# Paged attention with conditioned input: the second tile's mix and key projection moved ahead of the third query projection, its spreads and the output weights put in other slots

## The chip, the cores and the metric

The kernel runs on one core of one Trainium2 chip. A core has a matrix engine (TensorE, PE in the profile, with its weight loads as PEld), a vector engine (DVE), a scalar engine (ACT), GpSimd (POOL) and a sync engine (SP) that here only issues transfers. Each has its own instruction queue, and semaphores tie them together. The metric is the device time of one execution in microseconds; less is better.

## The reference

The input x has 64 sequences of 32 tokens with 512 features. The reference adds two residual branches. In the first, each sequence picks one of 16 matrices of 32 x 32 by its condition, and its 32 tokens are mixed with it:

```python
W = weights[condition]
x = x + einsum('bct,bcd->bdt', x, W)
```

The second is attention with a paged cache, 32 query heads and 8 key/value heads of 128 elements, 512 cached positions per sequence:

```python
q, k, v = x @ Wq.T, x @ Wk.T, x @ Wv.T         # 32, 8 and 8 heads
q, k = rope(rmsnorm(q, q_norm_w), pos), rope(rmsnorm(k, k_norm_w), pos)
k_all = concat(k_cache[block_table], k)         # 512 cached + 32 new keys
v_all = concat(v_cache[block_table], v)
o = softmax(mask(q @ k_all.T / sqrt(128))) @ v_all
x = x + o @ Wo.T
```

All is in float32.

## The kernel before, in words

The 2048 tokens are cut into 16 tiles of 128 tokens, which are four sequences ("batches" in the code) each. The heads are cut into two halves of 4 key heads and 16 query heads. So there are 32 steps, `steps[0]` to `steps[31]`: tiles 0 to 15 for the first half, then the same tiles for the second half (steps 16 to 31; the texts call them tiles 16 to 31). In the first half a step mixes its tile (`x1_c`, a matmul with the block-diagonal `bd`, and an add into `acc`), transposes it (`x1_b`) and stores the transposed tile `x1t` in DRAM; in the second half it is loaded again (`x1_t`).

From `x1t` come five kinds of projection, each of eight matmul instructions of 512 columns (`project`, line 401): one for the keys (`k_a`), one for the values (`v_a`) and four for the queries (`q_a`, one for each key head of the half). `norm_rope` then normalizes and rotates on ACT (square), DVE (six operations) and POOL (a power), with tables made by `rot_tables` from `cos` and `sin`. `angles` makes the latter for two tiles at a time, on DVE and ACT; its sine takes another function table on ACT than the exponential. The result goes into `rows`. For the first tile PE transposes `rows` into `q_cols` and `q_last` (`q_b`, `k_b`), and ACT copies; for all others DVE turns the rows (line 451) and SP spreads them by transfers within the chip's buffer (`spread`, line 465, four transfers per batch). `q_cols` holds batches 0 to 2 of a tile and `q_last`, of which there are two, batch 3.

For each batch, SP loads 16 key pages (`load_k`, line 291, two buffers), POOL gathers the values (line 315), DVE or ACT copies the keys of one head together (`head_keys`, `kh`), PE computes scores (line 570), ACT the exponential `pr`, and PE the values' sum (line 628). The 32 new keys of each sequence are done for a whole tile: `new_scores` (line 588, `psn`), their exponential `pn` on ACT, and `new_values` (line 612, `pnv`), which ACT copies into `nv`. `turn` (line 659) turns the finished batch into `ot`, and `out_proj` (line 516) multiplies it with the output weights `wo`, in slots 8 and 9 of the next tile.

A tile has 16 slots, four batches times four heads. A slot takes PE about 1.8 us with scores and values alone, and about 5.2 us with a projection. In each slot the loop of lines 901 to 976 also does a piece of the next tile, by the table of `pieces`, and loads weights part by part. The order of instructions of SP and PE is the order of the program throughout (line 88). In the opening, up to line 859, that holds for all engines; behind it a scheduler orders DVE, ACT and POOL. The opening computes the first tile's projections, the first batch and the start of the second, and puts the second tile's first pieces between them.

Buffers that matter here: the projections' PSUM pool `ps_p` has four buffers, used in turn by all that is named "pp" (mix, transposes, projections, new scores, new values, output projection). Every wait of a transfer issued by SP or ACT includes one for the transfer eight places earlier, since eight semaphores are used in turn.

Of the kernel before, what the change touches and what calls it, by code (L numbers as in the profile page):

```python
# [19 lines left out]
P = 128  # L20
# [7 lines left out]
BT = P // S  # L28
# [27 lines left out]
def cond_resid_paged_attention_kernel(  # L56
# [130 lines left out]
    def steps_of(exact, pools):  # L187
# [148 lines left out]
        class Step:  # L336
            def __init__(self, n):
                self.n, self.hh, self.t = n, n // NT, n % NT
                self.name = f"{n}_{uid}"

        def x1_a(st):

            st.acc = work.tile([P, HID], F32, tag="acc", name=f"acc_{st.name}", bufs=3)
            src = acc_d[st.t] if st.hh else x[st.t * P : (st.t + 1) * P, :]
            nc.sync.dma_start(st.acc, src)
# [14 lines left out]
        def x1_b(st):  # L360
            if st.hh:
                return
            pm = ps_p.tile([P, KC, P], F32, tag="pp", name=f"px1t_{st.name}")
            for c in range(KC):
                nc.tensor.transpose(pm[:, c, :], st.acc[:, c * P : (c + 1) * P], ident)
            st.x1t = work.tile([P, KC, P], F32, tag="x1t", name=f"x1t_{st.name}", bufs=1)
            nc.scalar.copy(st.x1t, pm)
            nc.scalar.dma_start(x1t_d[st.t], st.x1t.rearrange("p c q -> p (c q)"))

        def rot_tables(st):  # L370

            st.rot = {}
            c, s = cos[:, st.t, :], sin[:, st.t, :]
            for name, w in norm_w.items():
                cw = work.tile(
                    [P, 2, HD],
                    F32,
                    tag=f"cw_{name}",
                    name=f"cw_{name}_{st.name}",
                    bufs=1,  # L380
                )
                sw = work.tile(
                    [P, 2, HD],
                    F32,
                    tag=f"sw_{name}",
                    name=f"sw_{name}_{st.name}",
                    bufs=1,
                )
                w1, w2 = w[:, 0:HD], w[:, HD:D]
                nc.gpsimd.tensor_tensor(cw[:, 0, :], w1, c, ALU.mult)  # L390
                nc.gpsimd.tensor_tensor(cw[:, 1, :], w2, c, ALU.mult)
                nc.vector.scalar_tensor_tensor(
                    sw[:, 0, :], w2, -1.0, s, ALU.mult, ALU.mult
                )
                nc.gpsimd.tensor_tensor(sw[:, 1, :], w1, s, ALU.mult)
                st.rot[name] = cw, sw
# [379 lines left out]
        load_w("q", 0, 1, eng=nc.gpsimd)  # L776
        batch = Batch(first, 0)
        load_w("q", 0, 2)
        load_w("v", 0)
        x1_a(second)  # L780
# [28 lines left out]
        trig = work.tile([P, 3, TRIG * HD], F32, tag="w1", name="trig1", bufs=1)  # L809
        angles(TRIG, trig)  # L810
# [5 lines left out]
        q_a(first, 1)  # L816
        q_b(first, 0)
        head_keys(batch, 0, nc.scalar)
        head_keys(batch, 1, nc.scalar)
# [5 lines left out]
        k_b(first)  # L825
        for c in (0, 1):
            batch.fill(c)
            fetch(1, c)
        v_a(first)
        q_b(first, 1)  # L830
        x1_c(second)
# [7 lines left out]
        x1_b(second)  # L839
# [3 lines left out]
        rot_tables(second)  # L843
        k_a(second)
        q_b(first, 3)
        v_a(second)
# [4 lines left out]
        values(batch, 1)  # L851
        new_values(first, 2)
# [8 lines left out]
        def pieces(st):  # L861
            do = {
# [10 lines left out]
            if st is second:  # L873
                do[2] = do[3] = do[13] = ()
            return do
# [10 lines left out]
        new_ot(first)  # L886
# [13 lines left out]
        load_cond_weights(2)  # L900
        for st in steps:
# [3 lines left out]
            for bt in range(0 if st.n else 1, BT):  # L905
# [5 lines left out]
                for g in range(GH):  # L911
# [16 lines left out]
                    if slot == 9:  # L928
                        if st.n:
                            new_ot(st)  # L930
# [24 lines left out]
                    if st.t < 2:  # L955
                        load_parts([("o", i) for i in range(GH)], st.hh, slot - 10 + st.t * BT * GH)
# [95 lines left out]
```

## Time and profile before

| what | value |
|---|---|
| median of three runs | 2204.2 us (2204.06 to 2207.32) |
| the profiled execution's own time | 2204.06 us |
| its span from first to last instruction | 2202.3 us |
| PE busy | 2156.6 us (98%) |
| DVE, ACT, POOL busy | 1198.1, 867.5, 806.1 us |
| mean granted clock of PE | 0.991 of full speed |
| key loads `k_t` | 2048 of 64 KB |
| output weight loads `wo` | 32 of 256 KB |
| moved by all transfers | 358.77 MB, 163 GB/s over the span |

In a line of waits, the columns are the engine and what it wanted to run, what released it, and then the total in us, the number of waits and the longest. In a timeline line, the columns are the start in us, the duration (or how long a group of equal instructions lasted), the engine, the line of the code, the operation, its output and inputs, and how many; square brackets hold the idle time just before and what ended it. SPq is the queue of SP, which issues transfers. Names end in x where the program numbers them.

### The profile page before, as it was taken

The page shows a single profiled execution, that of the slowest core. Times are in us where ns is not written, and L with a number is a line of the kernel's source. Part 1 is how long each engine was busy: PE and PEld are TensorE (multiplying, and loading weights), DVE is VectorE, ACT ScalarE, POOL GpSimd, SP SyncE. Part 2 cuts the span into 40 slices and gives each one's busy share as a digit, 9 for nine tenths or more (in the row PEclk, how much of TensorE's full clock was granted, in tenths as well). Part 3 has the DMA queues.
Part 4 walks back from the last instruction along what each step waited for, and adds up shares of the span by engine and source line. Part 5 has one row for each costly group of instructions (what it writes and reads, how often), then busy time and mean ns, then how long its engine had stood idle before and what let it go on. Part 6 is the DMA issues. An engine that isn't in the chain of part 4 may idle for free.

```text
span 2202.3 us, 41557 instructions
## 1 busy us (share of the span) xinstructions
PE 2156.6 (98%) x12970; PEld 1502.4 (68%) x12970; DVE 1198.1 (54%) x2881; ACT 867.5 (39%) x1574; POOL 806.1 (37%) x1008
## 2 busy tenths in 40 slices
PE   8889999999999999999999999999999999999998
PEld 5657766677766777666776567776667776667775
DVE  5545466655555654565554555445656445656442
ACT  3424444444333444333433244333334433334441
POOL 4423243333333433333333343334333334334330
PEclk9989999999999999999999999999999999999999
DMA  7575554555555555556766655655555655555551
GB/s 226 160 177 168 159 155 143 165 157 171 155 151 151 158 168 162 154 147 197 238 176 174 165 167 162 176 158 154 148 163 163 174 159 158 149 162 158 174 158 55
DMA packets 387863, 358.77 MB, mean 163 GB/s; under 512 B 54737, under 2 KB 316897, under 8 KB 387633
## 3 DMA queue, kind: packets, MB, share of 16 engines
q1 hardware_dynamic: 342912, 215.10, 34.9%
q0 software_dynamic: 41712, 136.66, 20.9%
q10 hardware_dynamic: 3008, 4.25, 0.5%
q8 instruction: 106, 1.74, 0.3%
q14 instruction: 125, 1.02, 0.2%
HBM read 302.59 MB, written 12.58 MB: 143 GB/s over the span
## 4 chain that ended last, share of the span: by engine, by line
PE 93%; DMA 3%; SPq 2%; issue 1%; ACT 1%; DVE 0%; POOL 0%; DVEq 0%; ACTq 0%; POOLq 0%
PE po_x L628 20%; PE pout_x L516 20%; PE ps_x L570 20%; PE pp_q_x L401 19%; PE pp_k_x L401 5%; PE pp_v_x L401 5%; PE pnv_x L612 2%; PE psn_x L588 1%; SPq L291 1%; DMA k_t_x<-in_kt_dram 1%; PE pmix_x L357 1%; DMA raw_x<-in_vc_dram,v_row 0%; DMA x1t_d<-x1t_x 0%; DMA x1t_x<-x1t_d 0%; DMA wq_x<-in_wq_dram 0%
## 5 line engine op out<-in xcount | busy, mean ns | idle before, releaser
L315 POOL DMA_INDIRECT raw_x<-in_vc_dram,v_row x512 | 538.8, 1052 | 837.9 <-ACT v_x L328 769.3
L578 ACT ACTIVATE pr_x<-ps_x 128x512 f32<-128x512 f32 x512 | 305.8, 597 | 837.4 <-PE ps_x L570 774.4
L628 PEld LDWEIGHTS po_x<-v_x,pr_x 128*128 128x128 f32 x4096 | 516.5, 192 | 125.5 <-issue 114.8
L628 PE MATMUL po_x<-v_x,pr_x 128*128 128x129 f32 x4096 | 551.8, 278 | 0.9 <-ACT v_x L328 0.6
L401 PE MATMUL pp_q_x<-wq_x,x1t_x 128*128 128x512 f32 x1024 | 465.0, 597 | 2.8 <-DMA wq_x<-in_wq_dram 2.8
L516 PE MATMUL pout_x<-wo_x,ot_x 128*128 128x512 f32 x1024 | 451.6, 594 | 0.0
L570 PE MATMUL ps_x<-q_cols_x,kh_x 128*128 128x128 f32 x3072 | 408.7, 276 | 14.2 <-DVE kh_x L563 13.7
L570 PEld LDWEIGHTS ps_x<-q_cols_x,kh_x 128*128 128x128 f32 x3072 | 378.7, 193 | 31.9 <-issue 26.4
L328 ACT ACTIVATE v_x<-raw_x,valid 128x512 f32<-128x512 f32 x512 | 363.0, 716 | 11.6 <-DMA raw_x<-in_vc_dram,v_row 11.2
L516 PEld LDWEIGHTS pout_x<-wo_x,ot_x 128*128 128x128 f32 x1024 | 190.5, 191 | 215.1 <-issue 214.9
L401 PEld LDWEIGHTS pp_q_x<-wq_x,x1t_x 128*128 128x128 f32 x1024 | 186.5, 192 | 189.6 <-issue 186.4
L563 DVE COPY kh_x<-k_t_x 128x512 f32<-128x512 f32 x506 | 205.2, 417 | 181.4 <-PE ps_x L570 151.2
L646 DVE TENSOR_TENSOR nv_x<-po_x,nv_x 128x258 f32<-128x258 f32 x256 | 108.4, 423 | 341.3 <-PE po_x L628 319.9
L418 POOL TENSOR_TENSOR rs_q_x<-ms_q_x,minus_half 128x4 f32<-128x4 f32 x128 | 140.4, 1097 | 176.3 <-DVE ms_q_x L416 176.3
L411 ACT ACTIVATE sq_q_x<-pp_q_x 128x512 f32<-128x512 f32 x128 | 76.6, 598 | 273.6 <-PE pp_q_x L401 186.7
L570 PE MATMUL ps_x<-q_last_x,kh_x 128*128 128x128 f32 x1024 | 135.3, 275 | 0.0
L524 DVE TENSOR_TENSOR acc_x<-pout_x,acc_x 128x512 f32<-128x512 f32 x32 | 22.1, 692 | 200.2 <-PE pout_x L516 200.2
L570 PEld LDWEIGHTS ps_x<-q_last_x,kh_x 128*128 128x128 f32 x1024 | 124.6, 192 | 0.0
L401 PE MATMUL pp_k_x<-wk_x,x1t_x 128*128 128x512 f32 x256 | 117.7, 603 | 3.1 <-DMA x1t_x<-x1t_d 3.0
L415 DVE TENSOR_REDUCE ms_q_x<-sq_q_x 128x4 f32<-128x512 f32 x128 | 86.5, 676 | 54.4 <-ACT sq_q_x L411 52.7
L401 PE MATMUL pp_v_x<-wv_x,x1t_x 128*128 128x512 f32 x256 | 115.2, 592 | 0.0
L649 DVE TENSOR_TENSOR o_x<-nv_x,rden 128x256 f32<-128x256 f32 x256 | 108.5, 424 | 6.5
(105 smaller groups left out, 1464.6 us busy)
## 6 DMA issues: line engine op xcount, KB each, us to landing
k_t_x<-in_kt_dram SPq DMA_DIRECT2D x2048, 64.0 KB
q_cols_x<-rows_x SPq DMA_DIRECT2D x372, 80.0 KB
q_last_x<-rows_x SPq DMA_DIRECT2D x124, 80.0 KB
raw_x<-in_vc_dram,v_row POOLq DMA_INDIRECT x512
wo_x<-in_wo_dram SPq DMA_DIRECT2D x32, 256.0 KB
acc_x<-in_x_dram SPq DMA_DIRECT2D x16, 256.0 KB
x1t_d<-x1t_x ACTq DMA_DIRECT2D x16, 256.0 KB
acc_d<-acc_x SPq DMA_DIRECT2D x16, 256.0 KB
```

What stands on the lines that cost most here:

```text
L315: nc.gpsimd.indirect_dma_start(out=raw.rearrange("p g d -> p (g d)"), out_offset=None, in_=vc, in_offset=bass.IndirectOffsetOnAxis(ap=v_ro ...
L328: nc.scalar.activation(v_bufs[b % 2][:, c, :, 0:D], raw, AF.Copy, scale=ok)
L401: nc.tensor.matmul(pp, st.x1t[:, c, :], w[:, c, :], start=(c == 0), stop=(c == KC - 1))
L415: nc.vector.tensor_reduce(ms, sq, AX.X, ALU.add)
L418: nc.gpsimd.tensor_tensor(rs, ms, minus_half, ALU.pow)
L516: nc.tensor.matmul(st.po, st.ot[:, i, :], wt["o", st.hh, i // 4][:, i % 4, :], start=(i == 0), stop=(i == QH - 1),)
L563: last["dve"] = nc.vector.tensor_copy(k, ba.k_raw[:, :, g, :]).ins
L570: nc.tensor.matmul(ps[:, c, :], ba.k[g][:, c * P : (c + 1) * P], queries(ba, g), start=True, stop=True,)
L578: last["act"] = nc.scalar.activation(pr, ps, AF.Exp, scale=SCALE).ins
L628: nc.tensor.matmul(ba.po[:, g % 2, :], ba.pr[g][:, c, :], ba.v_t[:, c, g, :], start=(c == 0), stop=(c == VC - 1),)
L646: nc.vector.tensor_tensor(t, ba.po, t, ALU.add)
L649: nc.vector.tensor_tensor(ba.o[:, both, :], t[:, :, 0:D], rd.unsqueeze(2).to_broadcast([P, 2, D]), ALU.mult,)
```

## The change

The load of the second tile's x is issued by POOL, ahead of two small loads there, in place of SP behind the value weights. In the opening, the second tile's mix goes between the second query projection's matmuls (now called `pp_q_opening`) and its norm; the first tile's key transposes move up; the second tile's transposes, its key rotation table and its key projection come before the third query projection. Its query projection 0 comes into the opening, in the place of its key projection, and its value projection moves behind `new_values(first, 0)` and the values of batch 0, head 1. The trigonometry of tiles 2 and 3 moves from the front of the opening to a place behind that query projection, ahead of the scores of head 3 and the new scores.

In the loop of tile 0, the second tile's query projections 1 to 3 are in slots 4 to 6, where 0 to 3 were in slots 4 to 7. Its spreads are of batches 0 and 3 in slot 7, 1 in slot 10 and 2 in slot 11; they were of 0, 1 and 3 in slot 9 and 2 in slot 11. The second tile's `x1t` uses the buffer of `ot`, and `ot` of the first tile is allocated in slot 9. The output weights' eight parts, two loads of 256 KB each, were loaded in slots 10 to 15 of tiles 0 and 16 and slots 0 and 1 of tiles 1 and 17, one part a slot. Now a table gives the slots. All later tiles keep their order.

```diff
-        def x1_a(st):
+        def x1_a(st, eng=nc.sync):
...
-            nc.sync.dma_start(st.acc, src)
+            eng.dma_start(st.acc, src)
...
-            st.x1t = work.tile([P, KC, P], F32, tag="x1t", name=f"x1t_{st.name}", bufs=1)
+            if st.n == 1 and not exact:
+                whole = act.tile([P, QH, P], F32, tag="ot", name="x1t_second", bufs=1)
+                st.x1t = whole[:, 0:KC, :]
+            else:
+                st.x1t = work.tile([P, KC, P], F32, tag="x1t", name=f"x1t_{st.name}", bufs=1)
...
-        def rot_tables(st):
-
-            st.rot = {}
+        def rot_tables(st, kinds=("q", "k")):
+
             c, s = cos[:, st.t, :], sin[:, st.t, :]
-            for name, w in norm_w.items():
+            for name in kinds:
+                w = norm_w[name]
...
         load_w("q", 0, 1, eng=nc.gpsimd)
+        x1_a(second, nc.gpsimd)
         batch = Batch(first, 0)
         load_w("q", 0, 2)
         load_w("v", 0)
-        x1_a(second)
         load_w("q", 0, 3)
...
-        trig = work.tile([P, 3, TRIG * HD], F32, tag="w1", name="trig1", bufs=1)
-        angles(TRIG, trig)
...
         k_a(first)
-        q_a(first, 1)
+        pp = project(first, wt["q", 0, 1], "pp_q_opening")
+        x1_c(second)
+        finish(first, 1, pp, f"q_{first.name}_1", "q")
         q_b(first, 0)
+        k_b(first)
+        x1_b(second)
         head_keys(batch, 0, nc.scalar)
+        rot_tables(second, ("k",))
+        k_a(second)
         head_keys(batch, 1, nc.scalar)
         q_a(first, 2)
...
-        k_b(first)
         for c in (0, 1):
             batch.fill(c)
             fetch(1, c)
+        q_b(first, 1)
         v_a(first)
-        q_b(first, 1)
-        x1_c(second)
...
         q_b(first, 2)
-        x1_b(second)
         scores(batch, 2)
         head_keys(later, 0, nc.scalar)
         head_keys(later, 1, nc.scalar)
-        rot_tables(second)
-        k_a(second)
+        rot_tables(second, ("q",))
+        q_a(second, 0)
         q_b(first, 3)
-        v_a(second)
+        trig = work.tile([P, 3, TRIG * HD], F32, tag="w1", name="trig1", bufs=1)
+        angles(TRIG, trig)
         scores(batch, 3)
         new_scores(first)
         scores(later, 0)
         new_values(first, 0)
         values(batch, 1)
+        v_a(second)
         new_values(first, 2)
...
         def pieces(st):
-            do = {
+            if st is second:
+                return {
+                    4: ((q_a, 1),),
+                    5: ((q_a, 2),),
+                    6: ((q_a, 3),),
+                    7: ((spread, (0, 3)),),
+                    10: ((spread, (1,)),),
+                    11: ((spread, (2,)),),
+                }
+            return {
...
-            if st is second:
-                do[2] = do[3] = do[13] = ()
-            return do
...
-        new_ot(first)
...
+        output_weights = {
+            (0, 4): (0, 1),
+            (0, 5): (2, 3),
+            (0, 6): (4, 5),
+            (1, 4): (6,),
+            (1, 5): (7,),
+            (NT, 10): (0,),
+            (NT + 1, 2): (1,),
+            (NT + 1, 4): (2,),
+            (NT + 1, 5): (3, 4),
+            (NT + 1, 6): (5, 6),
+            (NT + 1, 7): (7,),
+        }
...
-                        if st.n:
-                            new_ot(st)
+                        new_ot(st)
...
-                    if st.t < 2:
-                        load_parts([("o", i) for i in range(GH)], st.hh, slot - 10 + st.t * BT * GH)
+                    for at in output_weights.get((st.n, slot), ()):
+                        load_parts([("o", i) for i in range(GH)], st.hh, at)
```

More of the change, by code (lines that the diff above doesn't have):

```diff
@@ L339, in __init__ @@
                 self.name = f"{n}_{uid}"
-        def x1_a(st):
+                self.rot = {}
+        def x1_a(st, eng=nc.sync):
             st.acc = work.tile([P, HID], F32, tag="acc", name=f"acc_{st.name}", bufs=3)
             src = acc_d[st.t] if st.hh else x[st.t * P : (st.t + 1) * P, :]
-            nc.sync.dma_start(st.acc, src)
+            eng.dma_start(st.acc, src)
         def x1_t(st):
```

## The prediction

> **What bounds the kernel now.** The page comes first: TensorE (PE) is busy 2156.6 of 2202.3 us, so only its idle time and its slow-clock time can be won. The table of PE's waits over the span says where it stood; the columns are total us, times, longest.
>
> ```profile
> PE ps_x L570 <- DVE kh_x L563: 13.7, 4, 4.8
> PE psn_x L588 <- DMA q_cols_x<-rows_x: 8.8, 1, 8.8
> PE pp_k_x L401 <- DMA x1t_x<-x1t_d: 3.0, 1, 3.0
> PE pp_q_x L401 <- DMA wq_x<-in_wq_dram: 2.8, 1, 2.8
> PE pnv_x L612 <- ACT nv_x L620: 1.0, 1, 1.0
> ```
>
> PE's timeline puts each at its place (start, us):
>
> ```profile
> 29.39 6.71 PE L401 MATMUL pp_q_x<-wq_x,x1t_x 128*128 128x512 f32 x8 [2.82 <-DMA wq_x<-in_wq_dram]
> 37.26 3.60 PE L401 MATMUL pp_v_x<-wv_x,x1t_x 128*128 128x512 f32 x8
> ...
> 112.49 0.39 PE L588 MATMUL psn_x<-q_cols_x 128*32 128x128 f32 x1 [8.77 <-DMA q_cols_x<-rows_x]
> ...
> 130.54 1.61 PE L570 MATMUL ps_x<-q_cols_x,kh_x 128*128 128x128 f32 x8 [3.07 <-DVE kh_x L563]
> ...
> 158.20 1.88 PE L570 MATMUL ps_x<-q_cols_x,kh_x 128*128 128x128 f32 x8 [4.83 <-DVE kh_x L563]
> ...
> 1210.08 5.17 PE L401 MATMUL pp_k_x<-wk_x,x1t_x 128*128 128x512 f32 x8 [3.01 <-DMA x1t_x<-x1t_d]
> ...
> 1240.97 2.04 PE L570 MATMUL ps_x<-q_cols_x,kh_x 128*128 128x128 f32 x8 [4.84 <-DVE kh_x L563]
> ```
>
> So every stall lies in the opening, in tile 0/1, or where the second half of the heads begins (tiles 16 and 17). After each gap the matmuls run at half speed for a while (6.71 against 3.60 for one projection). SP's timeline shows what the transfers were behind:
>
> ```profile
> 93.09 4.85 SPq L465 DMA_DIRECT2D q_cols_x<-rows_x  x8
> 97.99 4.07 SPq L465 DMA_DIRECT2D q_last_x<-rows_x  x4
> 102.10 1.07 SPq L249 DMA_DIRECT2D wo_x<-in_wo_dram  x2
> 103.27 3.07 SPq L465 DMA_DIRECT2D q_cols_x<-rows_x  x4
> 110.61 0.88 SPq L249 DMA_DIRECT2D wo_x<-in_wo_dram  x2
> 112.78 8.75 SPq L291 DMA_DIRECT2D k_t_x<-in_kt_dram  x16
> ```
>
> The output weights (16 loads of 256 KB a half) stand between the spreads and the key loads, in slots of 1.8 us where the transfers are 86 to 96% busy. In the order of instructions each load by SP or ACT also waits for the eighth before it, so a slow one holds SP.
>
> [...] gaps of 2.8 to 8.8 us were all followed by slow matmuls, costing 1.6 to 3.1 us each. [...] the row at 37.83 has 1.28, and the exponential starts at 39.12, so I take 1.28.
>
> **The change part by part.** No matmul is added or removed; only waits and slow clock count. Times "now" are worked out from rows of before.
>
> *a. Ahead of the third query projection.* Before lost 2.8 idle and 3.1 slow. Now the second tile's mix, first key transposes, second tile's transposes (px1t) and key projection stand there. But the projection pool has four PSUM buffers, and px1t is the fourth allocation after pp_q_opening, so it waits until DVE has read that for the rotation. DVE starts the first chain about 1.4 us sooner, as the trigonometry of tiles 2 and 3 is gone from its path (reduce at 21.37 before, about 19.9 now); POOL's pow, queued behind four gathers now 0.8 later (one more issue on POOL, 0.82), ends that chain at 24.15. A chain is 3.67 (21.37 to 25.04): key rows at 27.9, mix add 0.69 to 28.6, second query to its ropeu 2.2 to 30.9. PE is through at 28.45: it waits 2.4, transposes 0.5, waits 0.85 for ACT's copy. Matmuls pause from 27.0 to 32.2, so I charge a slow clock of 2.0 (bounds 0 and 3.1, the dearest row). The third projection then ends at 32.2 + 3.44 + 3.44 + 2.0 = 41.1. Before it ended at 35.94, and the work moved ahead of it is 0.86 + 0.43 + 0.43 + 3.44 = 5.2, that is 41.1: nothing won, nothing lost (2.0 won to 1.1 lost).
>
> *b. Up to the second tile's first query projection.* After that projection ACT has a square 0.6, two key copies 1.1, table 1.28, exponential 0.6, two value copies 1.35 and the query copy before the next scores, and key transposes and mix no longer fill PE's wait: 1.6 lost (0 to 3).
>
> *c. The moved trigonometry.* ACT's order is now: square of that query, table, sine, abs, cosine, table, exponential (batch 0, head 3), exponential pn. The sine waits on DVE, where the angles stand behind this query's chain and transpose. From the projection's end Y: square to Y+0.75, chain 3.67 and transpose to Y+5.25, seven DVE steps 2.05 (17.83 to 19.88) to Y+7.35, three ACT steps 0.95, table 1.28, two exponentials to Y+10.85. PE meanwhile has transposes, scores, new scores and scores: Y+4.3. The pnv matmuls of line 612 wait for pn: 6.6 us. Value projection and all values queue behind it. A slow clock follows, 2.3 (1.6 to 3.1), and 0.7 for the vn copy replaces the old 0.95. Loss 8.8. The opening thus loses 0 + 1.6 + 8.8 = 10.4, and the values that stood at 64.61 stand at 64.61 + 3.44 (the query moved in) + 10.4 = 78.5.
>
> *d. Spreads of tile 1.* The last query projection now falls in slot 6 and ends at 78.5 + 1.0 + 3 x 5.22 - 1.8 = 93.4; its rows are turned 6.0 later (84.70 to 91.06 before), 99.4. SP's order there is: batch 3's keys from about 75 to 83, twelve output-weight loads (3.1 MB, at some 280 GB/s gone by 97), eight spreads 4.85, the 16 loads of batch 4's keys 8.3, eight spreads 4.85: 117.4, landed about 3.4 later (bounds 2 and 6.2, the latter from 106.3 to 112.49 before): 120.8. PE, without slot 7's projection, gets there at 113.6. So 7.2 us of stall remain of 8.8, on kh for batch 4 and on psn together: what is late next is the key load behind the early spread.
>
> *e. Tile 1.* Key loads of batches 5 to 7 follow at once (125.7, 134, 142.5), ahead of their scores at 136 and 157; four output-weight loads land by 147, ahead of slot 9. The waits 3.07 and 4.83 and their slow clock (1.8 and 1.9) and 0.6 for a late value copy go: 12.2. With 1.6 from d that is 13.8 won against 10.4 lost: 3.4 net. The other way round: before 112.49 to the output projection's slow end at 160.8; now 120.8 + 36.7 (the same stretch without those waits) = 157.5.
>
> *f. Second half.* Only two output-weight loads stay at slot 10 of tile 16, two at slot 2 of tile 17, and twelve in its slots 4 to 7 (20.9 us long, at 104 to 160 GB/s in other tiles' long slots; 3.1 MB more is 150 GB/s, where the slices reach 322). x1t comes before them; batch 7's keys precede the twelve; batch 8's follow at slot 8 as usual, with some 9 us to spare (in tile 16 the spreads are out at 1187.5 and psn comes at about 1197). Gone: 3.0 + 1.6, then 4.84 to 5.0 + 0.95 + 0.5, and 0.46 for pn: 11.5. I leave 1.0 for contention: 10.5 won (6 to 11.5).
>
> The wider pieces of the diff (ot allocated later, x1t of tile 1 in its buffer) cost nothing: the first turn into ot comes in slot 9, behind tile 1's last query in slot 6. If that query slipped, the turn would wait; nothing needs ot before tile 1's slot 8. From tile 2 to 15 and from 18 on the order is as before: 0.
>
> Sum 3.4 + 10.5 = 13.9. The profiled run took 2204.06 (span 2202.3 and 1.8 around it), beside a median of 2204.2: 2204.1 - 13.9 = 2190.2.
>
> **Rivals.**
> *The stall at psn goes too*: if rows, spreads and keys run some 7 us faster than in d, or the clock stays up in the opening, 7.2 + 2.5 + 2 more are won: 2178.5. For it: spreads begin earlier in slots. Against: SP's order puts 16 loads at 0.52 between them. Chance 0.12.
> *The opening costs more*: two slow stretches of a whole projection, as at 29.39 (3.1 each), and longer waits in b and c cost 9 more; 2199. It is the same mechanism at its upper bound. Chance 0.15.
> *Slower: the bundles of twelve starve what follows*. At rate r, 3.1 MB lasts B; tile 1's spreads slip when B passes 20, batch 8's keys in tile 17 likewise, so B of 27 us, 115 GB/s, eats the 13.9; at 100 GB/s (31.5 us, 11.5 late twice) the time is 2213. Before, loaded slices moved 200 to 320 GB/s; against it. Chance 0.07.
> *My own*: 0.66, 2184 to 2197. That the change does nothing is no case: the order of instructions differs on every engine.
>
> **How the numbers follow.** A measurement of this kernel tells 0.2%, 4.4 us, from no change. Faster are my case, the fast rival and 0.06 of the opening rival, whose 2199 lies at the bound: 0.84; within 0.2% the rest of it, 0.09; slower 0.07. The range, 2179 to 2201, holds my case, most of the opening rival and half of the fast one; 0.06 of the fast one, the slow one and some 0.05 of tails stay out.
>
> **What would show it.** Right: the wait on wq at 29 and those on kh within tile 1 gone, pnv waiting some 6.6 us on pn near 63 to 69, psn waiting near 115 to 121, no wait on x1t or kh at tiles 16 and 17. Wrong: psn without a wait (d), no pnv wait (c), or waits on v_x and kh behind wo (e, f).

## The result, and the profile after

The changed kernel takes 2201.5 us (median of 12 runs, 2198.7 to 2207.5), the kernel before 2203.5 (12 runs, 2198.9 to 2207.3) beside it. The ratio is 0.9994, with a 95% interval of 0.9984 to 1.0005: no difference that can be measured. The forecast was 2190.2 us, with a range from 2179 to 2201. The profiled execution of the changed kernel took 2206.2 us, with a span of 2204.4; it is one of the slower ones.

The table of PE's waits over the whole span, to be set beside that of before (total us, times, longest):

```profile
PE ps_x L575 <- issue: 15.9, 1, 15.9
PE pnv_x L617 <- ACT pn_x L601: 6.3, 1, 6.3
PE pp_k_x L406 <- DMA x1t_x<-x1t_d: 3.4, 1, 3.4
PE pt_x L450 <- DVE rows_x L442: 2.7, 1, 2.7
...
PE psn_x L593 <- DMA q_cols_x<-rows_x: 1.6, 1, 1.6
```

The wait on `wq` and those on `kh` are gone, and the wait of `pnv` for `pn` is there, as foretold. But before batch 4's scores PE stands for 15.9 us, and there is a wait on `x1t`. PE's timeline gives the places:

```profile
30.07 5.30 PE L406 MATMUL pp_k_x<-wk_x,x1t_second 128*128 128x512 f32 x8 [0.69 <-ACT x1t_second L372]
35.21 3.60 PE L406 MATMUL pp_q_x<-wq_x,x1t_x 128*128 128x512 f32 x8
...
66.35 1.25 PE L617 MATMUL pnv_x<-vn_x,pn_x 32*128 32x129 f32 x16 [6.29 <-ACT pn_x L601]
70.57 5.53 PE L406 MATMUL pp_v_x<-wv_x,x1t_second 128*128 128x512 f32 x8 [0.95 <-ACT nv_x L625]
...
130.09 2.05 PE L575 MATMUL ps_x<-q_cols_x,kh_x 128*128 128x128 f32 x8 [15.87 <-issue]
134.33 0.42 PE L593 MATMUL psn_x<-q_cols_x 128*32 128x128 f32 x1 [1.62 <-DMA q_cols_x<-rows_x]
...
1285.47 5.37 PE L406 MATMUL pp_k_x<-wk_x,x1t_x 128*128 128x512 f32 x8 [3.40 <-DMA x1t_x<-x1t_d]
```

"Issue" says that the profile knows no releaser for the longest wait of the kernel. SP's timeline of the same stretch shows what was late:

```profile
81.00 13.06 SPq L249 DMA_DIRECT2D wo_x<-in_wo_dram  x12
99.66 2.50 SPq L470 DMA_DIRECT2D q_cols_x<-rows_x  x4
102.21 16.16 SPq L470 DMA_DIRECT2D q_last_x<-rows_x  x4
119.64 8.14 SPq L291 DMA_DIRECT2D k_t_x<-in_kt_dram  x16
127.88 4.94 SPq L470 DMA_DIRECT2D q_cols_x<-rows_x  x8
```

Four spreads of equal size took 2.50 us, and the next four 16.16. All that stands behind them in SP's queue, batch 4's keys and the eight spreads that the new scores need, starts 14 us late. The table of SP's own waits between 70 and 175 us names the releaser:

```profile
SPq L470 <- DMA x1t_d<-x1t_x: 13.6, 1, 13.6
```

A spread reads `rows` and writes `q_last`; it has no business with the store of tile 2's transposed `x1t` in DRAM. The chain of work that ended last runs through just that store (start us, us, what; stretch from 96 to 140 us):

```profile
112.89 0.53 PE px1t_x L366 x4
...
113.94 0.58 ACT x1t_x L372
114.55 2.04 DMA x1t_d<-x1t_x
116.60 0.51 SPq L470
```

PE's transposes in slot 15 of tile 0, ACT's copy, the store, and only then the spread of slot 7. The order of instructions shows the tie. This is a listing of the built program, not a view of the trace. It gives the waits of SP and of ACT there: the engine, the place in its queue, the line, what the transfer writes, and the semaphores. DMAHW0 to DMAHW7 are the eight semaphores that SP's and ACT's transfers use in turn in this program:

```
SP   157 L249 wo2      waits DMAHW5
SP   158 L249 wo2      waits DMAHW7
SP   159 L249 wo2      waits DMAHW0
SP   160 L470 q_cols   waits DVE, DMAHW1, PE, Activation
...
SP   164 L470 q_last1  waits DMAHW5
SP   165 L470 q_last1  waits DMAHW6
ACT  101 L373 x1t_d2   waits DMAHW6, Activation
```

Between the tenth and the eleventh of the twelve weight loads, semaphore 6 went to the store, which ACT issues. The store itself runs far later than its turn, in slot 15. Eight places after it, the second spread of `q_last` takes semaphore 6 again and so has to wait for the store: it goes out at 116.60, where the store, 2.04 us from 114.55, ends.

### The profile page after: what moved, and what is told of

The parts are those of the page before. It is cut to its first block, busy times and chain, and to the rows that moved or that the text cites. A ratio compares the mean times of both kernels' runs of the same rounds, so it can differ in the third digit from the quotient of the medians.

```text
span 2204.4 us, 41551 instructions
## 1 busy us (share of the span) xinstructions
PE 2153.9 (98%) x12970; PEld 1499.6 (68%) x12970; DVE 1199.3 (54%) x2881; ACT 870.0 (39%) x1576; POOL 809.4 (37%) x1009
## 4 chain that ended last, share of the span: by engine, by line
PE 93%; SPq 1%; issue 1%; DMA 1%; DVE 1%; ACT 1%; POOL 0%; DVEq 0%; POOLq 0%; ACTq 0%
PE po_x L633 21%; PE pout_x L521 20%; PE ps_x L575 20%; PE pp_q_x L406 19%; PE pp_k_x L406 5%; PE pp_v_x L406 5%; PE pnv_x L617 2%; PE psn_x L593 1%; SPq L470 1%; SPq L291 1%; PE pmix_x L358 1%; DMA raw_x<-in_vc_dram,v_row 0%; DMA pages_at<-in_pages_v_dram 0%; PE px1t_x L366 0%; POOL raw_x L315 0%
## 5 line engine op out<-in xcount | busy, mean ns | idle before, releaser
L406 PE MATMUL pp_q_x<-wq_x,x1t_x 128*128 128x512 f32 x984 | 442.7, 592 | 0.0
L575 PE MATMUL ps_x<-q_cols_x,kh_x 128*128 128x128 f32 x3072 | 407.4, 276 | 17.8 <-issue 15.9
L406 PEld LDWEIGHTS pp_q_x<-wq_x,x1t_x 128*128 128x128 f32 x984 | 177.6, 190 | 176.9 <-issue 176.5
```

Of the source, the lines that this page charges most:

```text
L406: nc.tensor.matmul(pp, st.x1t[:, c, :], w[:, c, :], start=(c == 0), stop=(c == KC - 1))
L575: nc.tensor.matmul(ps[:, c, :], ba.k[g][:, c * P : (c + 1) * P], queries(ba, g), start=True, stop=True,)
```

## The experiments

Each kernel was timed beside the kernel before on one chip. That kernel's median was 2204.1 us in the first group of four, 2200.0 in the second, 2202.9 and 2201.7 in the last two groups of two, and each group ran on another chip, so kernels of different groups are compared by their ratios to it. A ratio's interval is that of 95%; 0.1% is 2.2 us. Places in a timeline come from one execution each. Where two kernels do the same work they can still differ by some us: the first projection of the opening starts between 13.5 and 16.9 us, and a late start is found in kernels of both kinds.

### The store issued by SP

The theory is the false wait. The rivals: the bundle of twelve weight loads slows the transfers behind it, or the order of spreads and keys is what is late.

```diff
-            nc.scalar.dma_start(x1t_d[st.t], st.x1t.rearrange("p c q -> p (c q)"))
+            eng = nc.sync if st.n == 2 and not exact else nc.scalar
+            eng.dma_start(x1t_d[st.t], st.x1t.rearrange("p c q -> p (c q)"))
```

> The changed kernel, with the store of the third tile's transposed x1t (tile 2) issued by SP at its place in slot 15 of tile 0, behind the keys of batch 5, in place of ACT. Theory: SP stood for 13.6 us in the spreads of tile 1 because its semaphore was the one that this store had taken, and the store waits for PE's slot 15. Then SP's wait goes, the second lot of spreads is out near 118, the new scores of tile 1 start near 121 in place of 136, the wait of 15.9 us before batch 4's scores falls to 2 to 6 us, and the time falls by 10 to 12 us. Rival, bandwidth: the twelve output-weight loads ahead made keys and spreads late; then SP's spreads are as late and the time stays within 2 us of the changed kernel's. Rival, order: 16 key loads between the two lots of spreads are what is late; the time also stays within 2 us.

Measured: 2190.1 us, ratio 0.9934 (0.992 to 0.9948). SP's timeline of this kernel:

```profile
80.92 11.44 SPq L249 DMA_DIRECT2D wo_x<-in_wo_dram  x12
99.33 2.50 SPq L471 DMA_DIRECT2D q_cols_x<-rows_x  x4
101.87 2.51 SPq L471 DMA_DIRECT2D q_last_x<-rows_x  x4
105.64 9.42 SPq L291 DMA_DIRECT2D k_t_x<-in_kt_dram  x16
115.16 4.98 SPq L471 DMA_DIRECT2D q_cols_x<-rows_x  x8
```

and PE's timeline:

```profile
118.94 2.05 PE L576 MATMUL ps_x<-q_cols_x,kh_x 128*128 128x128 f32 x8 [4.11 <-issue]
121.73 0.39 PE L594 MATMUL psn_x<-q_cols_x 128*32 128x128 f32 x1 [0.18 <-DMA q_cols_x<-rows_x]
...
157.70 7.03 PE L522 MATMUL pout_x<-wo_x,ot_x 128*128 128x512 f32 x16
```

The four spreads take 2.51 us, the last lot of spreads is out at 120.1 in place of 132.8, and the new scores are no longer at 134.3 but at 121.7. The weight loads and the order are unchanged, and PE, DVE and POOL run their instructions in the same order in both kernels, so both rivals fall. Between the two ratios lie 0.60%, some 13 us; between the medians 11.4. One transfer of 256 KB, issued by the other engine, decides the whole forecast gain.

### The trigonometry back in front

```diff
+        trig = work.tile([P, 3, TRIG * HD], F32, tag="w1", name="trig1", bufs=1)
+        angles(TRIG, trig)
         for c in range(RAW):
             fetch(0, c)
...
         q_b(first, 3)
-        trig = work.tile([P, 3, TRIG * HD], F32, tag="w1", name="trig1", bufs=1)
-        angles(TRIG, trig)
```

> The changed kernel with the trigonometry of tiles 2 and 3 back at the front of the opening. Theory: the wait of pnv for pn (6.3 us) and the slow projection behind it (1.9) go; the chain of the first query is up to 1.5 us later, so that the third projection pays 0 to 1.5. SP's false wait stays but ends as much earlier as PE reaches slot 15 of tile 0. In all 6.5 to 8 us less. Rival: what SP waits for is bound by transfers and not by PE, so that the 8 us come back as a longer wait before batch 4's scores (24 us): within 2 us of the changed kernel's.

Measured: 2197.3 us, ratio 0.9966 (0.9954 to 0.9978); by the ratios 0.28% or 6.2 us less than the changed kernel, a little under the theory's 6.5 to 8; the rival's 2 is excluded by the two intervals taken together. The trace shows less than that in this stage. The wait of `pnv` is gone, and in PE's timeline the value projection takes 3.70 us where it took 5.53:

```profile
65.47 3.70 PE L406 MATMUL pp_v_x<-wv_x,x1t_second 128*128 128x512 f32 x8 [0.95 <-ACT nv_x L625]
69.84 0.71 PE L617 MATMUL pnv_x<-vn_x,pn_x 32*128 32x129 f32 x10 [0.25 <-ACT vn_x L505]
...
95.34 1.16 PE L633 MATMUL po_x<-v_x,pr_x 128*128 128x129 f32 x8 [0.90 <-ACT pr_x L583]
100.88 1.37 PE L633 MATMUL po_x<-v_x,pr_x 128*128 128x129 f32 x8 [3.49 <-ACT pr_x L583]
125.67 2.05 PE L575 MATMUL ps_x<-q_cols_x,kh_x 128*128 128x128 f32 x8 [15.33 <-issue]
```

The last lot of `pnv` matmuls stands at 69.84 against 76.78, 6.9 us earlier. Batch 4's scores are only 4.4 earlier (125.67 against 130.09). Of the 2.5 us lost on the way, 1.9 are two waits of values for exponentials, 0.90 and 3.49 against 0.39 and 2.07. The wait for the store is still there and moves along with PE, as the theory said.

### The weights of tile 17 in slots 3 to 5

```diff
-            (NT + 1, 4): (2,),
-            (NT + 1, 5): (3, 4),
-            (NT + 1, 6): (5, 6),
-            (NT + 1, 7): (7,),
+            (NT + 1, 3): (2, 3),
+            (NT + 1, 4): (4, 5),
+            (NT + 1, 5): (6, 7),
```

> The changed kernel with the output weights of tile 17 moved from slots 4 to 7 to slots 3 to 5 (four loads each). Theory: x1t of tile 19 was loaded late because twelve weight loads stood just ahead of batch 72's keys; spread over slots 3 to 5, SP is back in step by slot 8, the wait of 3.4 us on x1t at 1285 and the slow matmuls behind it go: 4 to 5 us less. Rival: the keys of the next batch, now behind four weight loads in slot 3, come late in tile 17 instead, and the time is the same or some 2 us more.

Measured: 2203.6 us, ratio 0.9996 (0.9988 to 1.0004), the same as the changed kernel. The wait on `x1t` near 1285 is gone from the trace, but the kernel is not faster. In the profiled executions of other kernels with the unchanged table this wait is between 2.25 us (the table with the key copies ahead of the norms, below) and nothing (the old slots in the first half, and the table alone); with the store by SP it is 1.2. In none of the four traces with the weights in slots 3 to 5 is it there. So the wait comes in some executions of the unchanged table and not in others, and what it costs on average is lost in the spread of the runs. The profiled one, with 3.4 us and a projection of 5.37 behind, lies 4.7 us above the median. I had taken one execution's wait for the kernel's.

### The spreads together

```diff
-                    7: ((spread, (0, 3)),),
-                    10: ((spread, (1,)),),
+                    7: ((spread, (0, 3, 1)),),
```

> The changed kernel with the spread of batch 1 of tile 1 in slot 7 beside those of batches 0 and 3, so that only batch 2's four spreads stand behind the key loads. Theory of the false wait: the spread that waits for the store stays held until about 116.6, batch 4's keys follow four spreads later, so the wait before its scores grows by about 2.4 us and the time by 0 to 3 us. Rival, order: with fewer spreads behind the keys the new scores come 2 to 8 us earlier and the time falls by as much.

Measured: 2202.4 us, ratio 0.9994 (0.9986 to 1.0003): within the theory's 0 to 3, outside the rival's 2 to 8. In PE's timeline the wait before batch 4's scores has grown by 2.5 us, and that at the new scores is gone:

```profile
132.88 2.05 PE L575 MATMUL ps_x<-q_cols_x,kh_x 128*128 128x128 f32 x8 [18.36 <-issue]
```

The order of spreads and keys only moves the wait from one to the other.

### The old slots in the first half

```diff
-            (0, 4): (0, 1),
-            (0, 5): (2, 3),
-            (0, 6): (4, 5),
-            (1, 4): (6,),
-            (1, 5): (7,),
+            (0, 10): (0,),
...
+            (0, 15): (5,),
+            (1, 0): (6,),
+            (1, 1): (7,),
```

> The changed kernel with the first half's output weights back in slots 10 to 15 of tile 0 and 0 and 1 of tile 1; the second half keeps the new table. Here the semaphore of tile 2's x1t store is that of the tenth key load of batch 4, so SP should stand there until about 116.5. Theory: that stall stays, but only six key loads, eight spreads and two weight loads are behind it, so tile 1's new scores start near 129 to 131 in place of 136; against that batches 5 and 6's keys are again behind weight loads, and waits on kh with slow matmuls of 8 to 12 us come back in tile 1. In all 2 to 7 us slower than the changed kernel. Rival: the weights' new slots win nothing in the first half; then 5 to 6 us faster than the changed kernel.

Measured: 2205.2 us, ratio 1.0024 (1.0014 to 1.0034); 0.30% or 6.6 us more than the changed kernel, inside the theory's 2 to 7. PE's timeline has the waits of before again:

```profile
120.51 2.05 PE L575 MATMUL ps_x<-q_cols_x,kh_x 128*128 128x128 f32 x8 [8.73 <-issue]
127.00 0.61 PE L593 MATMUL psn_x<-q_cols_x 128*32 128x128 f32 x2 [3.87 <-DMA q_cols_x<-rows_x]
144.81 2.01 PE L575 MATMUL ps_x<-q_cols_x,kh_x 128*128 128x128 f32 x8 [3.07 <-DVE kh_x L568]
172.45 2.04 PE L575 MATMUL ps_x<-q_cols_x,kh_x 128*128 128x128 f32 x8 [4.83 <-DVE kh_x L568]
```

Here the store's semaphore falls on a key load, SP stands for 3.8 us there, and the wait at the start of tile 1 is 12.6 in place of 17.5. What is saved in tile 1 by the new slots, 3.07 and 4.83 and the slow matmuls behind (4.46 us for the projection at 146.61, in place of 3.60), is larger. So they do win in the first half.

### The second half's table alone, in the kernel before

```diff
-                    if st.t < 2:
-                        load_parts([("o", i) for i in range(GH)], st.hh, slot - 10 + st.t * BT * GH)
+                    if st.n < 2:
+                        load_parts([("o", i) for i in range(GH)], 0, slot - 10 + st.n * BT * GH)
+                    for at in {
+                        (NT, 10): (0,),
+                        (NT + 1, 2): (1,),
+                        (NT + 1, 4): (2,),
+                        (NT + 1, 5): (3, 4),
+                        (NT + 1, 6): (5, 6),
+                        (NT + 1, 7): (7,),
+                    }.get((st.n, slot), ()):
+                        load_parts([("o", i) for i in range(GH)], 1, at)
```

> The kernel before with one part of the change: the output weights of tiles 16 and 17 by the new table. The opening and the first half are as before. Theory: the waits on x1t at 1210 and kh at 1241 and their slow matmuls go, as in the changed kernel, where this part won 11.2 us up to tile 17's slot 8, and up to 4.7 is given back at 1285: 7 to 11 us faster than before. Rival: the win of the second half belongs to the phase in which the changed first half delivers its tiles; then 0 to 4 us.

Measured: 2188.3 us, ratio 0.9951 (0.9938 to 0.9965): 10.8 us faster by the ratio, at the upper end of the theory's range, with no wait of PE in the second half among the ten largest. These six lines give 10.8 of the 13.9 us that I had forecast for the whole. The whole change is 0.43% (9.5 us) slower than this part of it; the rest of the change, in the first half, costs that.

### The store by SP in the kernel before

The edit is that of the first experiment.

> The kernel before, with the store of tile 2's x1t issued by SP at its place in slot 15 of tile 0 in place of ACT. There the store's semaphore is held against a weight load, which waits 4.2 us (and 7 us lie between the spreads and it). Theory: the false wait costs in this kernel too; batch 5's keys come 4 to 6 us sooner, the first kh wait of tile 1 (3.1) and part of the second (4.8) go, and the time falls by 3 to 6 us. Rival: key loads there are bound by buffers of keys not yet copied, and the time stays within 2 us of before.

Measured: 2200.9 us, ratio 1.0003 (0.9995 to 1.0011). The rival holds in the time. The weight loads go out at 103.67 in place of 110.61 and the keys behind them at 106.04 in place of 112.78, but in PE's timeline the waits on `kh` in tile 1 are to the hundredth those of before:

```profile
127.26 1.56 PE L571 MATMUL ps_x<-q_cols_x,kh_x 128*128 128x128 f32 x8 [3.07 <-DVE kh_x L564]
154.91 1.81 PE L571 MATMUL ps_x<-q_cols_x,kh_x 128*128 128x128 f32 x8 [4.83 <-DVE kh_x L564]
```

The first of the keys goes out 6.7 us sooner and the last 2.4, and yet PE waits for the copies just as long as before. The wait on `x1t` near 1210, which is one for a transfer, was 3.01 us in the one trace and 4.10 in the other. So I guessed that the waits on `kh` are of another kind; the last two experiments go after that. The same false wait that costs 13 us in the changed kernel costs nothing here.

### All three edits together

> The changed kernel with all three: the store of tile 2's x1t by SP, the trigonometry of tiles 2 and 3 back in front, the weights of tile 17 in slots 3 to 5. Theory: the store wins 11.5 as alone; the trigonometry wins 4 to 7 on top, unless SP's queue (rows, 16 keys, eight spreads) is now what the new scores of tile 1 wait for; the weights some 0 to 2: 2180 to 2186. Rival: SP's queue is the bound, and the time is that of the store alone, 2188 to 2190.

Measured: 2181.3 us (2178.0 to 2182.3), with the kernel before at 2200.0; ratio 0.9911 (0.9898 to 0.9924). It beats both kernels, the changed one by 0.83%, some 18 us. Beyond the store alone (0.9934) it wins 0.23%, 5 us; as the weights' edit alone showed nothing, I put most of that down to the trigonometry, which was not separated here.

### The first half's weights in tile 1 as well

On top of the three edits, eight of the sixteen loads go from tile 0 to tile 1, which then has twelve, and in the second kernel the spreads are together too.

```diff
-            (0, 4): (0, 1),
-            (0, 5): (2, 3),
-            (0, 6): (4, 5),
-            (1, 4): (6,),
-            (1, 5): (7,),
+            (0, 4): (0,),
+            (0, 5): (1,),
+            (1, 3): (2, 3),
+            (1, 4): (4, 5),
+            (1, 5): (6, 7),
```

> The three edits together (store by SP, trigonometry in front, weights of tile 17 in slots 3 to 5), and the first half's output weights as in the second: two parts in slots 4 and 5 of tile 0, two each in slots 3 to 5 of tile 1. Theory: what is left in the first half is that the spreads of tile 1 wait 5.6 us for the twelve weight loads ahead and values wait 4.5 us for exponentials on an ACT held up by late gathers; with four loads ahead most of that goes, 3 to 6 us less than the three edits, 2176 to 2179. Rival: the twelve loads then stand ahead of keys in tile 1, where SP is a few us behind, and kh waits take the place: 0 to 5 us more than the three edits.

> As the one before, and the spread of batch 1 of tile 1 in slot 7 beside those of batches 0 and 3. Theory, with nothing held up by the store's semaphore: batch 4's keys come 2.4 us later and the new scores no earlier than their keys allow, so 0 to 3 us more than without it. Rival: the new scores' spreads are the last to land, and it is 1 to 3 us less.

Measured: 2189.9 us, ratio 0.9943 (0.993 to 0.9957), and with the spreads together 2190.3, ratio 0.9947 (0.9934 to 0.9961). The theory of the first misses: it is 0.32%, 7 us, slower than the three edits. The rival had the direction right, and the twelve loads ahead of the keys as the place, but not more than 5 us. Tile 0's output projection does start earlier, at 150.31 against 152.98. Then come a short wait that the profile puts down to a key load, and a long one of the mix that neither side had named, in PE's timeline of the first of the two:

```profile
163.88 3.67 PE L522 MATMUL pout_x<-wo_x,ot_x 128*128 128x512 f32 x8 [1.32 <-DMA k_t_x<-in_kt_dram]
186.34 2.04 PE L358 MATMUL pmix_x<-acc_x,bd 128*128 128x512 f32 x2 [6.43 <-issue]
```

SP's timeline has the load of that tile's x issued at 183.11, behind spreads that began at 170.38 and keys that began at 159.41; in the kernel of the three edits these began at 162.83 and 154.19. That the mix waited for this load is read from the order and the times. The two kernels agree within their intervals: here too the order of the spreads is worth nothing.

### The key copies ahead of the norms, in the kernel before

If the keys were there, what did `kh` wait for? DVE's timeline of the kernel before, where the wait of 4.83 us ends:

```profile
157.03 0.71 DVE L451 STREAM_TRANSPOSE rows_x<-rope_q_x 128x512 f32<-128x512 f32 x1
157.66 1.39 DVE L563 COPY kh_x<-k_t_x 128x512 f32<-128x512 f32 x4
```

All four copies of a batch come in one go, at once behind the last query's turn, with no idle time ahead of them. A new theory: the order that the scheduler gave DVE puts the copies behind the norms. This edit changes nothing but the orders of DVE, ACT and POOL, and SP's and PE's stay as they were; the second kernel adds the second half's table.

```diff
                     for piece in fill.get(slot, ()):
-                        if isinstance(piece, tuple):
-                            piece[0](ahead, piece[1])
-                        else:
-                            piece(ahead)
+                        with ExitStack() as order:
+                            if st.t == 1 and slot in (3, 5, 6, 7):
+                                order.enter_context(tc.issue_after(last["dve"]))
+                            if isinstance(piece, tuple):
+                                piece[0](ahead, piece[1])
+                            else:
+                                piece(ahead)
```

> The kernel before, with every load in its old slot; in tiles 1 and 17 the norms of slots 3, 5, 6 and 7 are ordered behind the key copies of the slots ahead on each engine, so that on DVE the key copies come before the norms in whose wake they stood. Nothing else is changed, SP's and PE's orders are the same. Theory: the waits on kh of 3.07 and 4.83 in tile 1 and 4.84 in tile 17 are no late transfers; the keys lie there, and the copies stand in DVE's fixed order behind norms of projections that PE does just ahead. Then all three go with the slow matmuls behind them (1.8, 1.9 and 1.5), the wait on x1t of 3.0 stays: 14 to 18 us faster than before. Rival, transfers: the keys come late behind the weight loads; then DVE stands for them, the norms are late too, and the time is within 3 us of before.

> The kernel before with the second half's table of output weights, and the same order of copies and norms in tiles 1 and 17. Theory of DVE's order: in tile 17 the table has already moved the copies, so only tile 1 is left to win, 3.1 and 4.8 with 3.7 of slow clock: 9 to 12 us on top of the table's 10.8, 2178 to 2182 with the kernel before at 2201. Rival, transfers: nothing on top, 2188 to 2190.

Measured: 2195.1 us, ratio 0.9962 (0.9948 to 0.9976), 8.4 us faster than before; with the table 2189.8, ratio 0.9939 (0.9923 to 0.9954), no more than 0.12% beyond the table alone, which these intervals don't tell from nothing. The mechanism is right: the waits of 3.07, 4.83 and 4.84 on `kh` are gone with every load in its old slot, and what is left of that kind is 0.5. Both forecast sizes are missed. DVE's timeline of the first, and then PE's:

```profile
127.20 1.10 DVE L563 COPY kh_x<-k_t_x 128x512 f32<-128x512 f32 x3 [3.96 <-DMA k_t_x<-in_kt_dram]
...
146.55 0.43 DVE L563 COPY kh_x<-k_t_x 128x512 f32<-128x512 f32 x1 [1.56 <-DMA k_t_x<-in_kt_dram]
```

```profile
149.81 7.03 PE L516 MATMUL pout_x<-wo_x,ot_x 128*128 128x512 f32 x16
...
185.08 2.05 PE L357 MATMUL pmix_x<-acc_x,bd 128*128 128x512 f32 x2 [7.12 <-issue]
```

Now DVE stands for keys, but for 4.0 and 1.6 us only, and PE does not wait: tile 0's output projection starts at 149.81 against 159.86. Then the mix of tile 3 stands for 7.12 us. SP issued that tile's x at 181.55, hardly sooner than the 182.64 of the kernel before, and in slot 8 of tile 16 PE is at 1165.76, where before it was at 1165.74. So in tile 1 the waits on `kh` were cover for SP's queue: take them away and PE comes upon the x load, by the same reading of order and times. In tile 17, from there to slot 8, 71.37 us against 77.07 are 5.7 won and kept.

## Why the prediction was wrong, by its steps

**a, right in its waits, short in its net.** The third query projection started at 35.21 and, at 3.44, ended at 38.65; I had 41.1. The waits I put at 2.4 and 0.85 are 2.70 and 0.69, and 5.30 against 3.60 is 1.7 of slow clock (granted 0.50 from 30.07 to 33.0, 1.00 from 34.0 on) where I charged 2.0. That the 0.5 us of transposes between the two waits belongs to the pause, as I counted it, was an estimate; the rows do not show it apart. So 2.5 us were won where I had nothing, just past my bound of 2.0. That isn't chance of one execution: the value projection behind it starts at 35.4 to 37.5 in the five traces with the old opening and at 38.4 to 40.0 in the five with the changed one and the trigonometry behind it, 2.75 later in the mean for 5.16 of work moved ahead of it, so 2.4 won. The first projection's start, 13.72 against 15.66 in these two traces, looks like the reason and is not: with a start at 16.89 (the old slots) the value projection came at 38.78. What the gain comes from was not separated.

**b, right.** From the value projection to the second tile's first query projection 1.1 us were lost, where I had 1.6: two waits on query copies, 0.62 and 0.67, against twice 0.23 before, and values that took 1.38 us in place of 1.06.

**c, right in the mechanism, short in size.** From the end of the second tile's first query projection (52.11 + 3.44) to `pnv` at 66.35 are 10.8 us; I had 10.85. The wait is 6.29 (6.6). The two table loads on ACT took 1.28 us each (at 56.95 and 63.92), as the one at 37.83 in the trace of before. For the slow clock I had 2.3 (1.6 to 3.1). The value projection alone lost 1.9, and `pnv` and the values ahead of it another 1.5 (1.25 and 2.09 us, where they took 0.73 and 1.16 before): 3.4 in all. The granted clock was 0.50 from 66.35 to 74.0 and 1.00 from 75.0 on; in the kernel before it was 1.00 from 58 to 64. A third wait on a query copy, 0.67, stands here too. The stage lost 10.7 in place of 8.8, and the terms that I listed add up to 8.65, not 8.8. Values came at 77.41, forecast 78.5: the opening lost 9.4 where I had 10.4. That this is so near is partly luck, as a won 2.5 more than I had and c lost 1.9 more. Taking the trigonometry out again gave back 6.9 of it there.

**d, wrong, and this decides it.** The end of the last query projection, forecast 93.4, was 92.3, and its rows, forecast 99.4, were turned at 99.5: 7.2 behind the projection, where I had 6.0 and my rows of before give 6.4. Then I wrote "eight spreads 4.85, the 16 loads of batch 4's keys 8.3, eight spreads 4.85: 117.4". The first term, 4.85, was 18.7 us (99.66 to 118.37), because the second half of it waited 13.6 us for the store of tile 2's `x1t`. This is the step that failed. I had written that loads by SP and ACT also wait for the eighth before them "so a slow one holds SP", and then added up SP's queue without looking up which transfer stood eight places ahead of each. The trace of the kernel before already shows such waits. In the table of SP's waits up to 230 us, key loads and weight loads stand for stores of `x1t`:

```profile
SPq L291 <- DMA x1t_d<-x1t_x: 7.6, 2, 7.0
...
SPq L249 <- DMA x1t_d<-x1t_x: 4.2, 1, 4.2
```

The trace of the changed kernel shows what such a wait does to SP's queue: one spread was issued at 102.21, the next at 116.60, and nothing between. So the new scores came at 134.3, not at 120.8. With the store moved they came at 121.7, and tile 0's output projection at 157.70; I had worked out 157.5. Here too errors cancel: SP's last spread was out at 120.1 there, 2.7 after my 117.4, and the scores followed 1.6 behind it, where I had 3.4. Of PE's stall 4.3 us were left (4.11 and 0.18), where I had 7.2.

**e, right in amount, wrong in the reason.** No wait on `kh` is left in tile 1; with the old slots 3.07 and 4.83 come back. But I had put these waits down to weight loads between spreads and keys. They went just as well with every load in its place and the copies ahead of the norms. The new slots act through that order. DVE's timeline of the kernel before, and then of the changed kernel, in slot 3 of tile 1:

```profile
128.13 0.69 DVE L415 TENSOR_REDUCE ms_k_x<-sq_k_x 128x4 f32<-128x512 f32 x1 [5.55 <-ACT sq_k_x L411]
...
130.07 1.09 DVE L563 COPY kh_x<-k_t_x 128x512 f32<-128x512 f32 x3
```

```profile
145.69 1.43 DVE L568 COPY kh_x<-k_t_x 128x512 f32<-128x512 f32 x4 [1.33 <-DMA k_t_x<-in_kt_dram]
149.91 0.69 DVE L420 TENSOR_REDUCE ms_k_x<-sq_k_x 128x4 f32<-128x512 f32 x1 [2.79 <-ACT sq_k_x L416]
```

The keys were copied behind the key norm, and now they are copied ahead of it; with the old slots the norm is first again (142.40, the copies at 144.34). The net of the first half, 3.4 won, became 9.6 lost: the first matmuls of slot 8 in tile 16 stand at 1175.34 against 1165.74. Between 3.4 won and 9.6 lost lie 13.0, against a miss of 13.5 at the new scores.

**f, right in amount.** From that point to slot 8 of tile 17 are 65.92 us against 77.07: 11.1 won, where I had 11.5 less 1.0. The new order of copies and norms alone wins 5.7 of it, the wait of 4.84 and what follows; that on `x1t` is one for a transfer, and stays at 2.75 until the weights are out of its way. That "from 18 on the order is as before: 0" missed a wait of 3.4 in the profiled execution. By the runs with slots 3 to 5 it isn't measurable in the median, as above; I left it out of the sum for a wrong reason, not for a wrong amount.

**The sum.** 13.9 less 13 for the false wait leaves 1; measured are 2.0 by medians and 1.3 by the ratio. With the false wait taken away the kernel takes 2190.1 us, where the forecast was 2190.2; the interval of that ratio is some 3 us to either side, so a match to 0.1 is chance, and errors of opposite sign cancel in the parts above. The sum without the false wait holds; not each of its parts does.

**The rivals.** My slow one, twelve weight loads that starve what follows, had the right place, behind the bundle in SP's queue, and the wrong cause: with the same bundle and no false wait the spreads were in time. What the bundle itself costs, perhaps some of the 2.5 us for which values wait for exponentials while it runs, was not separated. The opening's rival had it at 9 us more than my 10.4; it lost 9.4 in all. Nothing in my cases was a wait between two transfers that share no data, and so the range ended at 2201.0, just short of the median.

## What to carry to other kernels

In this program the transfers of SP and ACT draw their semaphores from one set of eight, and a spread stood 13.6 us for the store that had had its semaphore before, though they share no data. So after a change of order look up, for each transfer of the queue that sets the path, which one held its semaphore and when that one can run. Where a wait names a copy, look at what the copy stood behind on its own engine before blaming the transfer ahead of it. And try the parts of a change apart: six lines of this one were worth 10.8 us, and the rest took 9.5 back.

## What the runs showed of the hardware

Matmuls behind a gap of the same length are not always slow for as long. After 6.28 or 6.29 us without matmuls, `pnv` took 1.24 or 1.25 us and the values behind it 2.09 in all five traces with that gap, where the kernel before, without it, took 0.73 and 1.16. The value projection that follows took 5.44 to 5.60 us in four of them and 3.70 in one (spreads together); at a granted clock of 1.00, at 37.26 in the kernel before, it took 3.60. Of the changed kernel, one of the four, the granted clock is given under c. Here is the one with 3.70, in PE's timeline:

```profile
64.80 1.25 PE L617 MATMUL pnv_x<-vn_x,pn_x 32*128 32x129 f32 x16 [6.28 <-ACT pn_x L601]
69.02 3.70 PE L406 MATMUL pp_v_x<-wv_x,x1t_second 128*128 128x512 f32 x8 [0.95 <-ACT nv_x L625]
```

So in these five traces the cost of the slow stretch varied by some 1.9 us, with gaps that agree within 0.01 us. The reason is not shown.

Shorter gaps had slow matmuls behind them too. In the kernel before, after waits of 2.82, 3.01 and 3.07 us, a projection took 6.71, 5.17 and 4.87 us in place of 3.60; the granted clock was 0.50 from 29.39 to 32.8, from 1210.08 to 1213 and from 132 to 134.

A store of 256 KB by ACT took 2.04 us from issue to release of the waiting spread in the changed kernel. In the kernel before the same store was issued at 103.56, and the weight load that waits for it went out at 110.61, in a stretch in which the transfers were busy (a share of 0.96 and 249 GB/s from 103.56 to 110.61). SP's own wait there is 4.2 us. How much of the 7 us is the store itself was not separated.
